# Edge tiles turned on VectorE in square blocks instead of on TensorE, with own shares' sums in PSUM and strip heads added in parts

## The chip, the core and the metric

The kernel runs on one core of a Trainium2 chip (trn2). The core's engines each have a queue of their own: TensorE (PE for its matmuls, PEld for its weight loads), VectorE (DVE), ScalarE (ACT), GpSimd (POOL) and SyncE (SP). ACT and SP also issue plain DMAs; POOL issues the indirect ones, which gather rows by an index. The metric is the device time of one execution in microseconds (us). A single execution was also recorded by the profiler; all stages and rows below are from that one.

## The reference

A graph layer over N = 50,000 nodes and 1,650,000 edges (800,000 random edges, both ways, and one loop edge for each node), sorted by destination. A node has D = 160 numbers: 64 scalars and 32 vectors of three. An edge has four numbers `sh`.

```python
s, v = x[:, :64], x[:, 64:].reshape(n, 32, 3)
ss, vv = s[src], v[src]
e0, e1 = sh[:, 0:1], sh[:, 1:4]
out0 = C0 * (ss * e0 @ W1 + einsum('eui,ei->eu', vv, e1) * INV3 @ W2)
out1 = C1 * (p3(ss, e1, W3) + p4(vv * e0, W4) + p5(cross(vv, e1), W5))
m_agg = segment_sum(concatenate([out0, out1]), dst, n)
h = concatenate([m_agg[:, :64] @ Ws, m_agg[:, 64:] by Wv])
x = layernorm(x + (x + relu(h)))
```

All of this is linear in x[src] times one of the four numbers of `sh`. So the kernel sums, for each destination and each k of 0 to 3, sh_k * x[src], and multiplies the sums by four prepared 160x160 matrices (BWk) once for each node.

## The kernel before, in words

**Groups, pairs, chunks.** Edges are cut into groups of G = 6 x 128 edges in the order of their destinations. A group touches at most W = 32 neighbouring nodes. Two groups are a pair (PG = 2, twelve blocks of 128 edges). SG = 20 groups are a chunk of ten pairs. There are 105 chunks and 1,044 pairs.

**A pair.** `gather` (L351) issues on POOL one indirect DMA for each block of 128 edges: 128 rows of x into `xg`, by the indices `si`. `spread` makes on DVE a one-hot matrix of the 32 nodes (`hot`, L360) and its product with the four numbers (`ha`, L363). `group_sums` (L388) multiplies on PE: the 128 columns of `ha` (4 numbers x 32 nodes) by the gathered rows, summed in PSUM over the six blocks of a group. `turn_sums` turns these sums on DVE in square blocks of 32x32 (L400) and adds them into a strip of nodes, `ring` (L407). `xg` has four buffers of twelve blocks, so POOL can be up to 48 gathers ahead of PE.

**A chunk.** While the ten pairs of a chunk run, the next chunk's edges are brought in. `load` (L259) issues on ACT's queue one DMA that puts the chunk's 120 blocks of 128 edges into SBUF, a block on each partition, six numbers for each edge: source, destination, four of `sh`. (For the first five chunks three DMAs from the inputs, L265 to L267; their integers are turned into floats by ACT, L274.) `place` is a generator that is taken forward in steps between the pairs' instructions, from the fifth pair on. Its steps:

- DVE picks the destination of each group's first edge (`first`, L320), PE spreads it over the partitions by a matmul with ones (L322) into PSUM (`bank`), and DVE takes it from there (`baseB`, L324); `aim` (L286 to L297) makes from it where in the strip each group's sums go.
- PE turns the sources (L328) and the destinations (L329) into `bank`, and each of the four numbers (L333) into `pk`, by matmuls with the identity.
- DVE makes the gathers' indices `si` (L336) and the place of each edge's node in its group, `rel` (L339), from `bank`, and two checks (L343, L344).

So `place` goes from DVE to PE, to DVE, to PE, and back to DVE. Each engine works through its queue in order: an instruction that waits holds all behind it.

**Strips.** A strip (`ring`, 98 of them) has ND = 5 parts of TW = 768 node columns; each starts 512 nodes after the last. When a group is the first of a new strip, what lies past column 512 of the old strip is added to the head of the new one: one DVE addition over 5 x 256 columns, L404. Before a strip is used, `set_own` writes the loop edges' shares into it: it multiplies (L691) and sums (L693) each node's shares `sa` to one number `sr`, multiplies the node's row by it (L694, 1280 columns), and turns the product into the strip (L698).

**Nodes.** When all groups of a block of 128 nodes are done, `block` multiplies the strip by BWk on PE (`phb`, L707, five matmuls), and DVE and ACT add x, relu and normalise (L183 to L197, with ACT's root at L192).

**Packing.** The destinations' loop edges are taken out of the edge list by VectorE: sixteen packs of 128 rows of 790 edges (L476 to L620). Each is read by ACT's queue, shifted together on DVE, and stored by SP's queue row by row at computed addresses in `edges` and `selves`, which later chunks read. ACT copies (L484 to L486, L504) and DVE's L505 begin each pack.

**What orders the work.** The order within PE, DVE, ACT and SP is the program's own, written by hand in the loop over pairs: matmuls of a pair, and after each one a share of the queued tasks (`after_pair`, `work`) and of the pack's steps. DMAs of ACT and SP go over eight completion counters in turn, both queues in one count: each DMA waits for the DMA that had its counter before.

The quoted functions follow as the program stands, with the profile's line numbers.

Of the kernel before, what the change touches and what calls it, by code (L numbers as in the profile page):

```python
# [39 lines left out]
F32 = mybir.dt.float32  # L40
# [10 lines left out]
P = 128  # L51
# [52 lines left out]
def tile_gnn_resnorm(ctx: ExitStack, tc: tile.TileContext, x, src, dst, attr, W1, W2, W3, W4, W5, Ws, Wv, out, n_edges):  # L104
# [123 lines left out]
    with tc.tile_pool(name="once", bufs=1) as once, tc.tile_pool(name="raw", bufs=2) as rawp, \  # L228
# [17 lines left out]
        nc.vector.tensor_copy(slotsP, slots)  # L246

        dq, loads = nc.sync, nc.scalar
        begun = []

        def load(s):

            q = loads if s else dq
            g0 = s * SG
            n = (min(NG, g0 + SG) - g0) * G
            if g0 >= NH:
                p0 = g0 * G * P - EH
                r6 = rawp.tile([P, P, 2 + NK], F32, name="r6")
                q.dma_start(r6[:n].rearrange("u p c -> u (p c)"),  # L259
                             edges[0, p0 * (2 + NK):(p0 + n * P) * (2 + NK)].rearrange("(u q) -> u q", u=n))  # L260
                return s, n, None, r6[:n, :, 0], r6[:n, :, 1], r6[:n, :, 2:]
            e = slice(g0 * G * P, (g0 * G + n) * P)
            ri = rawp.tile([P, 2, P], I32, name="ri")
            ra = rawp.tile([P, P, NK], F32, name="ra")
            q.dma_start(ri[:n, 0, :], src1[e].rearrange("(u p) o -> u (p o)", p=P))  # L265
            q.dma_start(ri[:n, 1, :], dst1[e].rearrange("(u p) o -> u (p o)", p=P))
            q.dma_start(ra[:n].rearrange("u p k -> u (p k)"), attr[e].rearrange("(u p) k -> u (p k)", p=P))  # L267
            return s, n, ri, None, None, ra[:n]

        def cast(loaded):  # L270
            s, n, ri, sf, df, af = loaded
            if ri is not None:
                rf = rawp.tile([P, 2, P], F32, name="rf")
                begun.append(nc.scalar.copy(rf[:n], ri[:n]))  # L274
                sf, df = rf[:n, 0, :], rf[:n, 1, :]
            return s, n, sf, df, af
# [37 lines left out]
        def place(cast_):  # L314

            s, n, sf, df, af = cast_
            ng = n // G

            first = idxp.tile([P, SG], F32, name="first")
            nc.vector.tensor_scalar(first[:n], starts[:n], df[:, 0:1], None, op0=ALU.mult)  # L320
            yield 1
            nc.tensor.matmul(bank[:, 3, :ng], ones[:n], first[:n, :ng], start=True, stop=True)  # L322
            baseB = idxp.tile([P, SG], F32, name="baseB")
            nc.vector.tensor_scalar(baseB[:, :ng], bank[:, 3, :ng], float(N - 1), None, op0=ALU.min)  # L324
            aim(s, ng, baseB)
            yield 1
            pi = bank[:, 1:3, :]
            nc.tensor.transpose(pi[:, 0, :n], sf, ident[:n, :n])  # L328
            nc.tensor.transpose(pi[:, 1, :n], df, ident[:n, :n])  # L329
            yield 1.5  # L330
            pk = psK.tile([P, NK, P], F32, name="pk")
            for k in range(NK):
                begun.append(nc.tensor.transpose(pk[:, k, :n], af[:, :, k], ident[:n, :n]))  # L333
                yield 0.75
            si = idxp.tile([P, P], I32, name="si")
            nc.vector.tensor_scalar(si[:, :n], pi[:, 0, :n], 0.0, float(N - 1), op0=ALU.max, op1=ALU.min)  # L336
            rel = idxp.tile([P, P], F32, name="rel")

            nc.vector.scalar_tensor_tensor(  # L339
                rel[:, :n].rearrange("p (g j) -> p g j", j=G), pi[:, 1, :n].rearrange("p (g j) -> p g j", j=G),  # L340
                float(N - 1), baseB[:, :ng].unsqueeze(2).to_broadcast([P, ng, G]),
                op0=ALU.min, op1=ALU.subtract)
            nc.vector.tensor_reduce(extremes[:, 0, s:s + 1], rel[:, :n], axis=AX.X, op=ALU.min)  # L343
            begun.append(nc.vector.tensor_reduce(extremes[:, 1, s:s + 1], rel[:, :n], axis=AX.X, op=ALU.max))  # L344
            placed[s] = si, rel, pk
# [50 lines left out]
        def turn_sums(p, ps):  # L396
# [4 lines left out]
            for i in range(ng):  # L401
                k = seg_of[g + i]
                if k and g + i == first_of[k]:
                    nc.vector.tensor_tensor(ring[k][:, :, :TW - S], ring[k][:, :, :TW - S], ring[k - 1][:, :, S:],  # L404
                                            op=ALU.add)
# [282 lines left out]
        def set_own(k, bs, got):  # L688

            xr, sa, nq = got  # L690
            nc.vector.tensor_tensor(sa[:, :nq], sa[:, :nq], quarter.unsqueeze(1).to_broadcast([P, nq, NK]), op=ALU.mult)  # L691
            sr = ownp.tile([P, BP * P // W], F32, name="sr")
            nc.vector.tensor_reduce(sr[:, :nq], sa[:, :nq], axis=AX.X, op=ALU.add)  # L693
            nc.vector.tensor_tensor(xr[:, :nq], xr[:, :nq], sr[:, :nq].unsqueeze(2).to_broadcast([P, nq, D]), op=ALU.mult)  # L694
# [23 lines left out]
        starts = once.tile([P, SG], F32, name="starts")  # L718
        nc.gpsimd.iota(starts, pattern=[[G, SG]], base=0, channel_multiplier=-1, allow_small_or_imprecise_dtypes=True)
        nc.vector.tensor_scalar(starts, starts, 0.0, None, op0=ALU.is_equal)  # L720
# [14 lines left out]
        nc.vector.scalar_tensor_tensor(quarter, quarter, float(W), of_k, op0=ALU.is_lt, op1=ALU.mult)  # L735
# [333 lines left out]
```

## Time and profile before

| what | value |
|---|---|
| time, median of 9 runs | 18,972.84 us (18,937.79 to 18,985.79) |
| profiled execution, its own time | 18,977.5 us |
| its span, first to last instruction | 18,975.8 us, so 1.7 us lie around it |
| mean granted TensorE clock in it | 0.611 |
| DVE busy | 7,102.3 us, 11,647 instructions |
| ACT busy | 224.4 us, 479 instructions |
| DMA | 805,153 packets, 1,339.61 MB, mean 71 GB/s |
| PE busy in `place`: L322, L328, L329, L333 (100 chunks) | 59.6, 46.2, 39.6, 138.0 us |
| DVE: turning of the pair's sums, L400 | 1,043 of 320 columns, 508 ns each |
| DVE: addition into the strip, L407 | 2,087 of 160 columns, 328 ns each |
| DVE: strip's head, L404 | 97 of 1,280 columns, 1,473 ns each |

How to read it: busy times are of one engine each and lie beside each other, so they don't add up to the span. What counts is which engine's queue is never ahead of the others, and what ends its waits. In a timeline a row has its start, its length, the engine, the line, the operation, out<-in and shapes; in brackets stand the engine's idle time before the row and what released it. "issue" means that nothing in the profile explains the idle time, "remote" that the releasing event has no instruction beside it.

### The profile page before, as it was taken

The numbers are of one execution on the slowest core, as the hardware profiler recorded it, in microseconds if no ns is written. First come the engines' busy times: TensorE is split into PE (matmuls) and PEld (weight loads), VectorE is DVE, ScalarE is ACT, GpSimd is POOL, SyncE is SP. The second block draws the span as 40 slices with busy tenths as digits, with TensorE's granted clock in tenths as the row PEclk, the third lists the DMA queues.
The fourth block names the chain that finished last, engine by engine and source line by source line (L and its number), as shares of the span: only waits on it lengthen the run. The fifth ranks groups of instructions, "written<-read, shape, count | busy, mean of one in ns | idle before, by whom it ended". The sixth has DMA issues, their size and how long they took to land. (4 is left out here: it accounts for less than half of the span.)

```text
span 18975.8 us, 100935 instructions
## 1 busy us (share of the span) xinstructions
PE 6943.1 (37%) x29811; PEld 5884.6 (31%) x29812; DVE 7102.3 (37%) x11647; ACT 224.4 (1%) x479; POOL 12067.8 (64%) x12536
## 2 busy tenths in 40 slices
PE   3333343333333334343433434334343333433333
PEld 3233232323323233332333323233232332323333
DVE  5342534325243343433425234252342534325223
ACT  0000000000000000000000000000000000000000
POOL 6566565665656566565665656666566665666666
PEclk6666666666566665666666666566565666656666
DMA  2222222222222222222222222222222222222222
GB/s 70 66 73 75 67 71 72 70 75 67 69 69 73 71 69 72 70 74 69 70 74 71 72 68 73 69 70 72 68 74 71 71 70 69 73 69 71 70 72 65
DMA packets 805153, 1339.61 MB, mean 71 GB/s; under 512 B 255167, under 2 KB 559476, under 8 KB 800610
## 3 DMA queue, kind: packets, MB, share of 16 engines
q0 software_dynamic: 601056, 1026.60, 20.6%
q10 hardware_dynamic: 192525, 267.12, 5.3%
q1 hardware_dynamic: 11017, 39.39, 0.6%
q8 instruction: 238, 3.90, 0.1%
q14 instruction: 317, 2.60, 0.0%
HBM read 1260.80 MB, written 71.40 MB: 70 GB/s over the span
## 5 line engine op out<-in xcount | busy, mean ns | idle before, releaser
L351 POOL DMA_INDIRECT xg<-in_x,si x12522 | 12064.0, 963 | 6886.8 <-issue 3663.5
L388 PE MATMUL ps<-xg,ha 128*128 128x160 f32 x25044 | 6185.8, 375 | 8958.2 <-issue 8314.4
L388 PEld LDWEIGHTS ps<-xg,ha 128*128 128x128 f32 x25044 | 5046.2, 246 | 9816.3 <-issue 9187.5
L400 DVE STREAM_TRANSPOSE sums<-ps 128x320 f32<-128x320 f32 x1044 | 530.1, 508 | 6332.4 <-remote 3189.5
L363 DVE TENSOR_TENSOR ha<-hot,pk 128x1536 f32<-128x1536 f32 x1044 | 1830.0, 1753 | 50.7 <-DVE hot L360 9.5
L707 PE MATMUL phb<-BWk,ring 128*128 128x160 f32 (+1 forms) x3910 | 1192.8, 375 | 1179.7 <-issue 1176.0
L707 PEld LDWEIGHTS phb<-BWk,ring 128*128 128x128 f32 (+1 forms) x3910 | 881.4, 249 | 1299.2 <-issue 1297.4
L183 DVE SCALAR_TENSOR_TENSOR y<-phb,xt 128x160 f32<-128x160 f32 x391 | 124.5, 319 | 2731.1 <-remote 1363.8
L407 DVE TENSOR_TENSOR ring<-ring,sums 128x160 f32 x2087 | 684.4, 328 | 277.0 <-issue 191.7
L505 DVE TENSOR_TENSOR hit<-marks,prow 128x395 f32<-128x395 f32 (+1 forms) x32 | 27.0, 843 | 1675.3 <-ACT marks L504 1664.6
L360 DVE TENSOR_TENSOR hot<-bank,rel 128x384 f32<-128x384 f32 x1044 | 564.7, 541 | 0.0
L322 PE MATMUL bank<-first,ones 120*128 120x20 f32 (+1 forms) x210 | 60.2, 369 | 1295.5 <-DVE first L320 738.7
L698 DVE STREAM_TRANSPOSE ring<-xr 128x1280 f32<-128x1280 f32 x188 | 466.2, 2480 | 6.4
L322 PEld LDWEIGHTS bank<-first,ones 120*128 120x128 f32 (+1 forms) x210 | 48.4, 287 | 1341.8 <-DVE first L320 765.9
L568 DVE COPY_PREDICATED prow<-marks,prow 128x2370 f32<-128x2370 int32 (+8 forms) x160 | 444.6, 2779 | 1.1
L192 ACT ACTIVATE rstd<-mv,eps_t 128x1 f32<-128x1 f32 x391 | 115.1, 294 | 16990.9 <-DVE mv L187 7468.3
L568 DVE COPY_PREDICATED pra<-marks,pra 128x1580 f32<-128x1580 int32 (+8 forms) x160 | 305.3, 1908 | 0.0
L694 DVE TENSOR_TENSOR xr<-xr,sr 128x1280 f32<-128x1280 f32 x188 | 280.0, 1489 | 6.9 <-issue 0.4
L328 PE MATMUL bank<-ident,r 120*128 120x120 f32 x100 | 46.5, 465 | 548.6 <-issue 272.7
L328 PEld LDWEIGHTS bank<-ident,r 120*128 120x128 f32 x100 | 21.1, 211 | 574.2 <-issue 284.1
L197 DVE TENSOR_SCALAR o<-y,mv,rstd 128x160 f32<-128x160 f32 x391 | 146.0, 373 | 17.7 <-DVE rstd L196 1.5
L404 DVE TENSOR_TENSOR ring<-ring 128x1280 f32<-128x1280 f32 x97 | 142.9, 1473 | 1.8
(354 smaller groups left out, 2337.9 us busy)
## 6 DMA issues: line engine op xcount, KB each, us to landing
xg<-in_x,si POOLq DMA_INDIRECT x12522
xr<-in_x ACTq DMA_DIRECT2D x748, 160.0 KB
edges<-prow SPq DMA_DIRECT2D x1994, 18.5 KB
r<-edges ACTq DMA_DIRECT2D x99, 360.0 KB
selves<-mine SPq DMA_DIRECT2D x1992, 0.5 KB
xt<-in_x ACTq DMA_DIRECT2D x195, 160.0 KB
out<-o ACTq DMA_DIRECT2D x195, 160.0 KB
pra<-in_attr ACTq DMA_DIRECT2D x15, 1580.0 KB
```

The source lines that it names most:

```text
L197: nc.vector.tensor_scalar(o[:n], y[:n], mv[:n, 0:1], rstd[:n], op0=ALU.subtract, op1=ALU.mult)
L351: nc.gpsimd.indirect_dma_start(out=xg[:, j, :], out_offset=None, in_=x, in_offset=bass.IndirectOffsetOnAxis(ap=placed[0][:, u + j:u + j + ...
L360: nc.vector.tensor_tensor(hot[:, :n], slotsP[:, 0:W].unsqueeze(1).to_broadcast([P, n, W]), rel[:, u:u + n].unsqueeze(2).to_broadcast([P, n ...
L363: nc.vector.tensor_tensor(ha[:, :n], hot[:, :n].unsqueeze(2).to_broadcast([P, n, NK, W]), pk[:, :, u:u + n].rearrange("p k u -> p u k").un ...
L388: mm = nc.tensor.matmul(ps[:, j // G, :], ha[:, j].rearrange("p k w -> p (k w)"), xr, start=j % G == 0, stop=j % G == G - 1)
L400: nc.vector.transpose(at[:, :ng], ps[:, :ng].rearrange("p g (b f) -> p g b f", f=FB))
L404: nc.vector.tensor_tensor(ring[k][:, :, :TW - S], ring[k][:, :, :TW - S], ring[k - 1][:, :, S:], op=ALU.add)
L407: nc.vector.tensor_tensor(here, here, at[:, i], op=ALU.add)
L568: nc.vector.copy_predicated(what[:n, a:e], mi[:, r].unsqueeze(2).to_broadcast([n, e - a, what.shape[2]]), what[:n, a + d:e + d])
L694: nc.vector.tensor_tensor(xr[:, :nq], xr[:, :nq], sr[:, :nq].unsqueeze(2).to_broadcast([P, nq, D]), op=ALU.mult)
L698: nc.vector.transpose(ring[k][:, :, c0:c0 + nq * W].rearrange("p b (w q) -> p q b w", q=nq), xr[:, :nq].rearrange("p q (b f) -> p q b f", ...
L707: wrote("misc", nc.tensor.matmul(ph[:nb], ring[k][:, i, c0:c0 + nb], BWk[:, i, :], start=i == 0, stop=i == ND - 1))
```

## The change

- `load` brings each chunk into SBUF in another form. The chunk's rows are cut into 30 partitions of four blocks, and each block into four quarters of 32 edges; quarter i lies on the partitions from 32 i on, by a DMA of its own. A fifth to eighth DMA bring the destination of each group's first edge (20 numbers of four bytes each, on the partitions from 32 i on). So a chunk takes eight DMAs on ACT's queue where it took one (sixteen where it took three, for the first five chunks). The tiles are made once, two of each, and cleared at the start (ten memsets on DVE) instead of coming from a pool.
- `place` uses DVE alone: three square-block transposes (32 columns for the first edges into `baseB`, 256 columns for sources and destinations into `bank`, 512 for the four numbers into `pk`) take the place of the multiplication L320, the matmul L322 and the six PE transposes of L328, L329 and L333. Its steps weigh 3 instead of 6.5 in the share of the tasks.
- `set_own`: the mask `quarter` and the sums `sr` lie in PSUM, in unused columns of `bank` (`shareP`, `sumP`).
- `turn_sums`: the strip's head is added in five additions, one for each part, and only up to the last column that the old strip's groups can have written. By the plan's bounds this is 133 to 256 columns, 215 in the mean.

```diff
         def load(s):
-            q = loads if s else dq
+            qs = [loads] * NK if s else [dq, loads] * (NK // 2)
...
+            def fetch(to, what, c):
+                rows = what.rearrange("(l b q) -> l b q", l=nl, b=nb)
+                for i, q in enumerate(qs):
+                    q.dma_start(to(slice(i * W, i * W + nl)), rows[:, :, i * W * c:(i + 1) * W * c])
+            def fetch_first(to, what, at, c):
+                firsts = what.rearrange("(g q) -> g q", g=ng)[:, at:at + 1]
+                for i, q in enumerate(qs):
+                    q.dma_start(to[i * W:i * W + ng], firsts)
...
-                q.dma_start(r6[:n].rearrange("u p c -> u (p c)"), edges[...].rearrange("(u q) -> u q", u=n))
+                fetch_first(fd, e, 1, 2 + NK)
+                fetch(lambda r: r6[r, :nb].rearrange("l b e c -> l b (e c)"), e, 2 + NK)
...
         def place(cast_):
-            nc.vector.tensor_scalar(first[:n], starts[:n], df[:, 0:1], None, op0=ALU.mult)
-            yield 1
-            nc.tensor.matmul(bank[:, 3, :ng], ones[:n], first[:n, :ng], start=True, stop=True)
-            nc.vector.tensor_scalar(baseB[:, :ng], bank[:, 3, :ng], float(N - 1), None, op0=ALU.min)
+            nc.vector.transpose(baseB, fd.to_broadcast([P, W]))
+            nc.vector.tensor_scalar(baseB[:, :ng], baseB[:, :ng], float(N - 1), None, op0=ALU.min)
             aim(s, ng, baseB)
             yield 1
-            nc.tensor.transpose(pi[:, 0, :n], sf, ident[:n, :n])
-            nc.tensor.transpose(pi[:, 1, :n], df, ident[:n, :n])
-            yield 1.5
+            nc.vector.transpose(pi[:, :, :nb * W].rearrange("p c (l b) -> p c b l", b=nb), ef)
+            yield 1
-            for k in range(NK):
-                begun.append(nc.tensor.transpose(pk[:, k, :n], af[:, :, k], ident[:n, :n]))
-                yield 0.75
+            begun.append(nc.vector.transpose(pk[:, :, :nb * W].rearrange("p k (l b) -> p k b l", b=nb),
+                                             af.rearrange("p b e k -> p k b e")))
+            yield 1
...
         def turn_sums(p, ps):
-                    nc.vector.tensor_tensor(ring[k][:, :, :TW - S], ring[k][:, :, :TW - S], ring[k - 1][:, :, S:],
-                                            op=ALU.add)
+                    past = max(high[first_of[k - 1]:first_of[k]]) + W - k * S
+                    for b in range(ND):
+                        nc.vector.tensor_tensor(ring[k][:, b, :past], ring[k][:, b, :past], ring[k - 1][:, b, S:S + past],
+                                                op=ALU.add)
...
         def set_own(k, bs, got):
-            nc.vector.tensor_tensor(sa[:, :nq], sa[:, :nq], quarter.unsqueeze(1).to_broadcast([P, nq, NK]), op=ALU.mult)
-            nc.vector.tensor_reduce(sr[:, :nq], sa[:, :nq], axis=AX.X, op=ALU.add)
-            nc.vector.tensor_tensor(xr[:, :nq], xr[:, :nq], sr[:, :nq].unsqueeze(2).to_broadcast([P, nq, D]), op=ALU.mult)
+            nc.vector.tensor_tensor(sa[:, :nq], sa[:, :nq], shareP.unsqueeze(1).to_broadcast([P, nq, NK]), op=ALU.mult)
+            nc.vector.tensor_reduce(sumP[:, :nq], sa[:, :nq], axis=AX.X, op=ALU.add)
+            nc.vector.tensor_tensor(xr[:, :nq], xr[:, :nq], sumP[:, :nq].unsqueeze(2).to_broadcast([P, nq, D]), op=ALU.mult)
```

## The prediction, on record before the changed kernel ran

> **What bounds the kernel now.** First I read the page's busy times and its costliest groups, to find the engine that never rests long.
>
> ```profile
> PE 6943.1 (37%) x29811; PEld 5884.6 (31%) x29812; DVE 7102.3 (37%) x11647; ACT 224.4 (1%) x479; POOL 12067.8 (64%) x12536
> ...
> L351 POOL DMA_INDIRECT xg<-in_x,si x12522 | 12064.0, 963 | 6886.8 <-issue 3663.5
> L388 PE MATMUL ps<-xg,ha 128*128 128x160 f32 x25044 | 6185.8, 375 | 8958.2 <-issue 8314.4
> ```
>
> POOL is the busiest, and nearly all of it is the gather. Its plain step is the median gather, 949 ns (the gather's own view), and 0.30 us of "issue" before it (the timelines below): 12,522 x 1.2535 = 15,696 us. That is 83% of the span and no part of the change touches it. The other 3,280 us are what an edit can win: gathers that last longer, and idle time above 0.3 us. The waits of POOL name what ends its idle time:
>
> ```profile
> POOL xg L351 <- issue: 3663.5, 12010, 0.7
> POOL xg L351 <- PE ps L388: 2357.4, 235, 84.8
> POOL xg L351 <- remote: 762.7, 172, 8.6
> ```
>
> The 12,010 issues are the plain step. The rest is POOL without a free `xg` buffer, waiting for PE's sums. Sorted by length, fifteen gaps are 64 to 85 us each, 1,133 us in all; they lie at the beginnings of packs, where DVE's L505 waits for ACT, and ACT's DMAs wait for SP's row-by-row stores. The change leaves that chain in place. About 380 gaps of 0.4 to 20 us hold 1,942 us above the 0.3. PE is not short of peak work in them: its largest idle time is 8,314 us of "issue", a PE that goes forward one instruction in 0.7 or 1.4 us while POOL gathers and DVE rests. It is back at pace 3 to 5 us after POOL stops, which is why a gap costs 5 us on average.
>
> **Part 1: own shares' sums in PSUM, the strip head in parts.** A timeline shows what a long DVE addition does to a gather:
>
> ```profile
> 10440.51 0.94 POOL L351 DMA_INDIRECT xg<-in_x,si  x1 [0.30 <-issue]
> ...
> 10441.61 1.49 DVE L404 TENSOR_TENSOR ring<-ring 128x1280 f32<-128x1280 f32 x1
> 10441.76 2.17 POOL L351 DMA_INDIRECT xg<-in_x,si  x1 [0.30 <-issue]
> ...
> 10444.23 0.94 POOL L351 DMA_INDIRECT xg<-in_x,si  x1 [0.30 <-issue]
> ```
>
> The gather that starts inside L404 ends 0.83 us after it and lasts 2.17 instead of 0.95 us. I sorted all gathers by the DVE row in which they start. In L404, 100 slow gathers carry 63.1 us above 0.95; in L694, 184 carry 110.9. These two have both inputs in SBUF. The others show no such rows: 179 gathers start inside the turn L698, all near 0.95, and 69 lie over L582, which has an operand in PSUM, at 0.94 to 0.95. L407, of L404's kind but 328 ns, costs about nothing.
>
> ```profile
> L698 DVE STREAM_TRANSPOSE ring<-xr 128x1280 f32<-128x1280 f32 x187 | 464.9, 2486 | 6.4
> L694 DVE TENSOR_TENSOR xr<-xr,sr 128x1280 f32<-128x1280 f32 x187 | 279.2, 1493 | 6.8 <-issue 0.4
> L404 DVE TENSOR_TENSOR ring<-ring 128x1280 f32<-128x1280 f32 x97 | 142.9, 1473 | 1.8
> ```
>
> *L694 with an operand in PSUM* becomes L582's kind (1,800 ns for 1,580 columns, so about 1,458 for 1,280: DVE's own time stays). I take all of its **-111 us**; bounds 0 (POOL makes nothing of it) and -111. *L404 in five parts*: 215 columns take 0.25 us by L404's own rate (1.15 ns a column) and 0.44 by L407's (2.05). A gather started in a part is held by at most that, and one strip head falls on about one gather, so I leave 100 x 0.2 = 20 us of 63: **-43 us**; bounds 0 and -63. DVE's five parts take 1.25 to 2.2 us for 1.47.
>
> The Trainium skill ("SBUF — State Buffer", section "Who interferes with whom") says that an operation of VectorE with two SBUF inputs contends only with a GpSimd operation that reads SBUF, and reports a probe in which tensor_tensor did not stall DMAs. By that rule both edits would be worth 0, and the sum below 18,761. The 2.17 us row above, and its hundreds of like, speak for a hold; I go by the row.
>
> **Part 2: `place` without TensorE.** Now `place` goes DVE, PE, DVE, PE, DVE. In one chunk's timeline:
>
> ```profile
> 10719.13 0.95 POOL L351 DMA_INDIRECT xg<-in_x,si  x1 [0.30 <-issue]
> 10725.96 0.33 DVE L183 SCALAR_TENSOR_TENSOR y<-phb,xt 128x160 f32<-128x160 f32 x1 [22.64 <-remote]
> ...
> 10726.78 0.20 DVE L320 TENSOR_SCALAR first<-starts,r 120x20 f32<-120x20 f32 x1
> ...
> 10727.04 0.62 PE L322 MATMUL bank<-first,ones 120*128 120x20 f32 x2 [34.14 <-DVE first L320]
> ...
> 10732.03 0.95 POOL L351 DMA_INDIRECT xg<-in_x,si  x1 [11.95 <-PE ps L388]
> ```
>
> DVE waits 22.64 us in L183 for PE's `phb`, whose end reaches it late; `first` stands behind it; PE stands 34.14 us at L322 for `first` with gathered rows lying ready; POOL runs out of buffers and stops for 11.95 us. The view of L322 says how common that is:
>
> ```profile
> its engine sat idle before it (us, times) until:
>   DVE first L320: 1504.6, 103
> ```
>
> 15 us in each chunk, of which the buffers (48 gathers ahead) cover most. What POOL loses I get by sorting its gaps by the pair of the chunk: `place` runs while PE is at the fifth to eighth pair, and POOL, up to four pairs ahead, shows it in its last pair. That pair loses 390 us in 73 gaps over all chunks; the other nine lose 172 us on average. The excess is 218 us. Counted otherwise: the gaps in which PE's next work was L322, L328, L329 or L333, or DVE's next was L336, are 44 with 290 us; all gaps with any `place` row within 25 us are 93 with 480. I take **-220 us**; bounds 0 (the same slow PE makes POOL wait a little later) and -480.
>
> *What DVE gets for it*: transposes of 32 + 256 + 512 = 800 columns a chunk, at 1.59 ns a column (L400: 508/320) to 1.94 (L698: 2,486/1,280), so 1.3 to 1.6 us, less L320's 0.2; 105 chunks make 110 to 150 us more of DVE. DVE idles 62% of the span and POOL does not wait for `si` but for buffers: **0**. Without that cover it would be +150. The matmuls that go are 283 us of PE; PE isn't late by its work, 0.
>
> **Part 3: the loads.** One DMA a chunk becomes eight, all on ACT's queue ahead of whatever ACT does next. ACT's DMA rows in the same timelines take 0.33 to 0.56 us, 7 x 0.47 = 3.3 us a chunk. Behind them on ACT stands the root L192, on which DVE's L196 waits in order, and behind L196 the turning and `hot`, `ha` for PE. L192 is issued a pair ahead of L196, 12 x 1.2535 = 15 us, so 3.3 us hide: **0**. Bounds: 0 and the price in the fourth rival. The bytes are nearly the same, in 560 pieces a chunk in place of 120: some 46,000 more beside 805,153 packets, on DMA engines that the page shows two tenths busy: 0.
>
> **Part 4: start.** Ten memsets, 3,076 columns at L655's 0.88 ns (1,125/1,280), 2.7 us before the first load, against one iota less: **+3**; bounds 0 and +10 (sixteen DMAs for the first chunk, half on SP).
>
> **Sum**: -111 - 43 - 220 + 0 + 0 + 3 = -371. From the profiled execution's 18,977.5: **18,606 us**. That execution lies 4.7 us above the median of nine, which is nothing beside the bounds.
>
> **Rivals.**
>
> 1. *All the gaps near `place` go, and the hold wholly*: -480 - 111 - 63 + 3 = -651, 18,327. For it: once PE stays ahead, POOL's buffers start each pack fuller. Against it: other pairs lose 172 us each without `place`, so some of the 93 gaps are the ordinary kind. 0.07.
> 2. *Only the holds go.* PE still creeps while POOL gathers and DVE rests; the 34 us that it stood at L322 are then spent creeping, and POOL stops in the next pair. -111 - 43 + 3 = -151, 18,827. For it: DVE's L183 waits 22 us for `phb` in both kernels, and PE goes no faster for having no L322. Against it: the last pair's excess over the other nine. 0.24.
> 3. *The change does not do what it says* for time: the holds come from something that goes with L694 and L404, and the gaps come back: 18,940 to 19,015 (0.2%, 38 us, is about what a measurement of this kernel can tell from no change). 0.07.
> 4. *Slower: ACT is held by its own loads.* ACT's and SP's DMAs take eight counters in turn, and each waits for the one that had its counter before; in the program 313 of 872 load DMAs follow one of SP's, where it was 34 of 100. SP issues its stores every 0.7 to 2.1 us while POOL gathers. A load of eight then holds ACT 3.3 + 3 x 2.1 = 9.6 us. If L192 stands behind it and less than a pair of slack is left, DVE stops at L196, PE creeps on, and POOL stops; at half of 9.6 for each of 105 chunks that is +504, and it decides from the point where ACT's hold passes the 15 us between L192 and L196. Where it decides, the gains of part 2 are given back too: +504 - 151 = +353, 19,330; with part 2 kept, +133, 19,110. For it: L196 has waited 66.7 us for ACT once already. Against it: ACT is busy 1%, and its DMA waits are shorter than a pair nearly everywhere. 0.18.
>
> **How the numbers follow.** The forecast, 18,480 to 18,720 around 18,606, has 0.44, with rival 1 0.07, rival 2 0.24: faster 0.75. Within 0.2%: 0.07. Slower: 0.18. For 8 in 10 I leave out most of rival 1 below 18,390 and the dearer part of rival 4 above 19,060. The one-sign part (faster) reaches from 18,327 to 18,935.
>
> **What would show it.** Gathers over 0.98 us that start inside the own shares' product: 184 before, a few after; at strip heads about 100 with 0.2 us in place of 0.63. POOL's last pair of a chunk should lose about 172 us like the others, and no idle of PE should be put down to `place`. DVE should be 110 to 150 us busier, its first wait in `place` one for a DMA. I am wrong if POOL's waits for PE's sums keep their 2,357 us (rival 2), if DVE's L196 waits for ACT in many chunks or the transposes wait for their loads (rival 4), or if a gather's median moves from 0.949 or its issue from 0.30: a hundredth of a microsecond there is 125 us.

## The result, and the profile after

The changed kernel took 19,072.38 us (median of 10 runs, 19,038.28 to 19,111.52), the kernel before beside it 18,983.8 us (31 runs). The ratio is 1.0051, 95% interval 1.0043 to 1.0059: **0.5% slower** (89 us), where 2% faster was forecast. The profiled execution has a span of 19,087.7 us, 111.9 more than before; it lies 17 us above its median.

The page's busy times and costliest groups, as shown of before:

```profile
PE 6958.6 (36%) x28971; PEld 5891.2 (31%) x28972; DVE 7262.7 (38%) x12254; ACT 224.7 (1%) x484; POOL 11911.4 (62%) x12535
...
L376 POOL DMA_INDIRECT xg<-in_x,si x12522 | 11907.7, 951 | 7133.7 <-issue 3664.7
L413 PE MATMUL ps<-xg,ha 128*128 128x160 f32 x25044 | 6305.7, 379 | 10823.4 <-issue 10012.0
```

POOL is busy 156 us less (the holds, gathers that last longer beside a VectorE operation, are gone), and idles 247 us more. PE's idle time of "issue", most of it in slow stretches in which PE goes forward one instruction in 0.7 or 1.4 us, grew by 1,698 us. The waits of POOL:

```profile
POOL xg L376 <- issue: 3664.7, 12005, 1.8
POOL xg L376 <- PE ps L413: 2603.7, 270, 87.1
POOL xg L376 <- remote: 736.6, 169, 7.1
```

The wait for PE's sums, which was to shrink by some 220 us, grew by 246.

Every gather's length and the idle time before it can be sorted into classes that add up to the span: 12,522 plain steps (up to 0.949 us and 0.305 before it, some 15,679 us in both), what gathers last beyond that (holds), gaps of 0.4 to 20 us, the fifteen long gaps at the beginnings of packs, and the two ends.

| us | before | after | difference |
|---|---|---|---|
| holds | 201.0 | 43.8 | -157.2 |
| gaps of 0.4 to 20 us | 1,937.5 (380) | 2,115.4 (417) | +177.9 |
| holds and those gaps together | 2,138.5 | 2,159.2 | +20.7 |
| fifteen gaps at pack beginnings | 1,128.2 | 1,206.9 | +78.7 |
| ahead of the first gather | 8.4 | 12.5 | +4.1 |
| behind the last gather | 20.6 | 28.0 | +7.4 |
| plain steps and rest | 15,680.1 | 15,681.1 | +1.0 |

The holds went as forecast (154 us), and came back as gaps. What stays is the pack beginnings and the ends.

An own shares' product of the kernel after, in its timeline, beside two gathers:

```profile
3108.89 1.49 DVE L720 TENSOR_TENSOR xr<-xr,bank 128x1280 f32<-128x1280 f32 x1
...
3109.08 0.94 POOL L376 DMA_INDIRECT xg<-in_x,si  x1 [0.30 <-issue]
...
3110.33 0.95 POOL L376 DMA_INDIRECT xg<-in_x,si  x1 [0.30 <-issue]
```

With one operand in PSUM the same 1.49 us hold neither gather, and none of the 351 gathers that lie over such a product. So why did POOL not gain? A slow stretch of the kernel after shows it:

```profile
4847.20 0.38 PE L733 MATMUL phb<-BWk,ring 128*128 128x160 f32 x1 [0.45 <-issue]
...
4857.78 0.52 DVE L425 STREAM_TRANSPOSE sums<-ps 128x320 f32<-128x320 f32 x1 [9.36 <-PE ps L413]
...
4889.35 0.33 DVE L183 SCALAR_TENSOR_TENSOR y<-phb,xt 128x160 f32<-128x160 f32 x1 [30.33 <-PE ps L413]
...
4889.88 0.94 POOL L376 DMA_INDIRECT xg<-in_x,si  x1 [6.58 <-PE ps L413]
```

PE's last `phb` matmul begins at 4,847.20. DVE, which waits for it in L183, goes on at 4,889.35, 42 us later, and within a microsecond of that POOL is let go, after 6.58 us of rest. **PE's ends reach the other engines late, and they arrive when POOL rests.**

The trace also records PE's signals themselves, the updates of the semaphore that its matmuls raise. In this stretch none is recorded from 4,857.76 to 4,889.33, though eight matmuls that raise it end in between; then fourteen come 0.04 us apart, while POOL rests. The whole trace of before has 272 such bursts (five or more updates, each at most 0.06 us behind the one before), and 264 of them begin inside one of POOL's rests of over 0.4 us, 5.6 us after its start at the median; in the trace of after it is 302 of 303. So the lateness lies between a matmul's end and its signal, not in PE's work.

One can measure it for every pair whose turning DVE had to wait for: from the end of the pair's last matmul row to the start of the turning. The median is 24.5 us in the profile of before and 26.4 us in that of after. The prediction saw "whose end reaches it late" in one row and priced PE's slow pace instead.

### The profile page after: what moved, and what is told of

It reads as the page before. It is cut to its first block, busy times and chain, and to the rows that moved or that the text cites. A ratio compares the mean times of both kernels' runs of the same rounds, so it can differ in the third digit from the quotient of the medians.

```text
span 19087.7 us, 100631 instructions
## 1 busy us (share of the span) xinstructions
PE 6958.6 (36%) x28971; PEld 5891.2 (31%) x28972; DVE 7262.7 (38%) x12254; ACT 224.7 (1%) x484; POOL 11911.4 (62%) x12535
## 3 DMA queue, kind: packets, MB, share of 16 engines
q0 software_dynamic: 601056, 1026.60, 20.3%
## 4 chain that ended last, share of the span: by engine, by line
issue 45%; POOL 31%; PE 15%; another core or an unknown queue 5%; DMA 3%; DVE 1%; DVEq 0%; ACTq 0%; POOLq 0%; ACT 0%
POOL xg L376 31%; PE ps L413 13%; DMA xg<-in_x,si 3%; PE phb L733 2%; DVE prow L595 0%; DVE ha L388 0%; DVE mine L612 0%; DVE ring L434 0%; DVE pri L592 0%; DVE hot L385 0%; DVE sums L425 0%; DVE pri L590 0%; DVE marks L588 0%; DVE ring L724 0%
## 5 line engine op out<-in xcount | busy, mean ns | idle before, releaser
L376 POOL DMA_INDIRECT xg<-in_x,si x12522 | 11907.7, 951 | 7133.7 <-issue 3664.7
L413 PE MATMUL ps<-xg,ha 128*128 128x160 f32 x25044 | 6305.7, 379 | 10823.4 <-issue 10012.0
L413 PEld LDWEIGHTS ps<-xg,ha 128*128 128x128 f32 x25044 | 5181.6, 251 | 11764.4 <-issue 10977.8
L183 DVE SCALAR_TENSOR_TENSOR y<-phb,xt 128x160 f32<-128x160 f32 x391 | 124.7, 319 | 3593.5 <-PE ps L413 2430.9
L720 DVE TENSOR_TENSOR xr<-xr,bank 128x1280 f32<-128x1280 f32 x188 | 278.8, 1483 | 7.3 <-DVE bank L719 0.7
L431 DVE TENSOR_TENSOR ring<-ring 128x196 f32<-128x196 f32 (+20 forms) x485 | 149.1, 372 | 1.8
L185 DVE BATCH_NORM_STATS2 st<-y 128x6 f32<-128x160 f32 x391 | 128.0, 327 | 13.7 <-DVE y L183 0.4
L682 DVE MEMSET ring<- 128x1280 f32 (+1 forms) x98 | 119.3, 1218 | 23.5 <-issue 21.0
L592 DVE COPY_PREDICATED_SCALAR hit<-marks,none 128x395 int32 (+8 forms) x160 | 105.0, 656 | 10.6 <-DVE pri L590 4.7
L357 DVE STREAM_TRANSPOSE pk<-r 128x512 f32<-128x512 f32 x100 | 104.5, 1045 | 0.0
```

What stands on the lines that cost most here:

```text
L376: nc.gpsimd.indirect_dma_start(out=xg[:, j, :], out_offset=None, in_=x, in_offset=bass.IndirectOffsetOnAxis(ap=placed[0][:, u + j:u + j + ...
L413: mm = nc.tensor.matmul(ps[:, j // G, :], ha[:, j].rearrange("p k w -> p (k w)"), xr, start=j % G == 0, stop=j % G == G - 1)
L431: nc.vector.tensor_tensor(ring[k][:, b, :past], ring[k][:, b, :past], ring[k - 1][:, b, S:S + past], op=ALU.add)
L720: nc.vector.tensor_tensor(xr[:, :nq], xr[:, :nq], sumP[:, :nq].unsqueeze(2).to_broadcast([P, nq, D]), op=ALU.mult)
```

## Experiments

Theory A: POOL does not set the pace; what it wins it gives back in a wait. Theory B, the prediction's: POOL sets it, and holds are on the path. Theory C: the loads of eight DMAs cost time at the pack beginnings. Each group of runs was on one chip with its own runs of the kernel before, and differences are against those. In the third group the kernel before took 15,982 us in place of some 19,000, with the same program; that difference is a finding, told below. Of the kernel before there are two traces in all, the first one and r1, so the traces of the other groups are compared with a kernel before of another group.

| run | time, before beside it | ratio, 95% interval | holds | gaps of 0.4 to 20 | pack gaps | turning behind the last matmul, median |
|---|---|---|---|---|---|---|
| e1 | 19,067.2, 19,087.4 | 0.9990 (0.9979 to 1.0001) | 97 | 2,138 | 1,144 | 22.3 |
| e2 | 19,101.6, 19,087.4 | 1.0011 (1.0000 to 1.0021) | 151 | 2,088 | 1,130 | 23.6 |
| e3 | 19,186.1, 19,087.4 | 1.0052 (1.0038 to 1.0065) | 192 | 2,028 | 1,259 | 27.2 |
| e4 | 19,150.7, 19,087.4 | 1.0035 (1.0023 to 1.0048) | 198 | 2,056 | 1,182 | 23.9 |
| r1 | 19,013.4, 19,054.7 | one run | 207 | 1,990 | 1,128 | 23.6 |
| r2 | 19,122.9, 19,054.7 | 1.0039 (1.0025 to 1.0053) | 43 | 2,170 | 1,217 | 25.8 |
| e5 | 19,087.7, 19,054.7 | 1.0022 (1.0012 to 1.0031) | 39 | 2,199 | 1,169 | 26.4 |
| e6 | 19,316.9, 19,054.7 | 1.0145 (1.0127 to 1.0163) | 201 | 2,194 | 1,167 | 26.5 |
| e7 | 16,446.9, 15,982.0 | 1.0291 (1.0274 to 1.0309) | 699 | 50 | 0 | 0.04 |
| e8 | 15,954.1, 15,982.0 | 0.9983 (0.9973 to 0.9992) | 194 | 64 | 0 | 0.04 |
| e9 | 15,834.9, 15,982.0 | 0.9907 (0.9891 to 0.9924) | 39 | 90 | 0 | 0.04 |
| r3 | 19,162.9, 19,067.8 | 1.0048 (1.0034 to 1.0063) | 41 | 2,222 | 1,252 | 25.5 |
| e10 | 19,059.8, 19,067.8 | 0.9992 (0.9982 to 1.0001) | 602 | 1,631 | 1,139 | 26.5 |
| e11 | 19,041.9, 19,067.8 | 0.9989 (0.9977 to 1.0000) | 209 | 1,815 | 1,258 | 30.8 |
| e12 | 19,100.2, 19,067.8 | 1.0016 (1.0003 to 1.0028) | 47 | 1,992 | 1,306 | 35.7 |
| e13 | 18,995.0, 18,982.4 | 1.0007 (0.9997 to 1.0016) | 39 | 2,129 | 1,160 | 20.3 |
| e14 | 18,981.5, 18,982.4 | 0.9995 (0.9985 to 1.0004) | 199 | 1,950 | 1,115 | 24.7 |
| r4 | 19,080.1, 18,982.4 | 1.0046 (1.0032 to 1.0060) | 41 | 2,108 | 1,189 | 26.6 |

(us. Pack gaps: all gaps of 20 us and more; e3, r2, r3, e11 and e12 have a sixteenth, of 20 to 35 us, and e6 has 32.)

### The parts alone

**e1**, the kernel before with the own shares' sums (and their mask) in PSUM:

```diff
-            sr = ownp.tile([P, BP * P // W], F32, name="sr")
-            nc.vector.tensor_reduce(sr[:, :nq], sa[:, :nq], axis=AX.X, op=ALU.add)
+            nc.vector.tensor_reduce(sumP[:, :nq], sa[:, :nq], axis=AX.X, op=ALU.add)
```

> The kernel before with one edit: mask and sums of the own shares in PSUM. Both theories expect the own shares' product to hold no gather (111 us of excess in 184 gathers before, about 0 here). Theory A, given back: POOL is always let go by PE, so time that POOL wins at a hold is idle time at the next empty buffer; the gaps of 0.4 to 20 us grow from 1,942 by some 80 to 130 us and the time stays within 30 us of before. Theory B, the holds are on the path: the gaps stay within 40 us of 1,942 and the time falls by 90 to 120 us.

Measured: holds 97 us, 20 us faster, with 0 just inside the interval. A is closer; B's 90 to 120 us are out.

**e2**, the kernel before with strip heads in five additions:

```diff
-                    nc.vector.tensor_tensor(ring[k][:, :, :TW - S], ...
+                    for b in range(ND):
+                        nc.vector.tensor_tensor(ring[k][:, b, :past], ...
```

> The kernel before with one edit: strip heads added in five parts, up to the last column written. Both theories expect the excess of gathers at strip heads to fall from 63 to some 40 us. Theory A (given back): time within 25 us of before. Theory B (on the path): 15 to 45 us faster.

Measured: holds 50 us less than before's 201; the time 14 us longer, not shorter. B is out here too.

**e3**, the changed kernel with those two parts taken back (the diffs above, reversed):

> The changed kernel with own shares' sums and strip heads as before, so the new loads and the placing on VectorE alone. Theory A (holds are given back): 70 to 110 us slower than before, as slow as the whole change; gaps of 0.4 to 20 us near 1,950 to 2,050, the fifteen gaps at pack beginnings some 80 us longer in all. Theory B (the holds did pay 150 us, and the placing costs what hides that): about 240 us slower than before. A third, that the placing pays its 220 us and something in the other part costs: faster than before.

Measured: 99 us slower, as the whole change. A holds, B's 240 us are out, and so is the third, that the placing pays.

**e4**, the kernel before with seven DMAs more for each load, into tiles nobody reads:

```diff
+                    for i in range(NK):
+                        q.dma_start(fx[s % 2][i * W:i * W + ng], firsts)
...
+                for i in range(1, NK):
+                    q.dma_start(rx[s % 2][i * W:i * W + nl, :nb].rearrange("l b e c -> l b (e c)"), ...)
```

> The kernel before, with seven more DMAs at each load of a chunk from the sixth on (three quarters and four columns of first edges, into a scratch tile that nothing reads). Theory C, the loads hold ACT at the beginnings of packs, where POOL already stands: the fifteen gaps there grow from 1,128 by 60 to 90 us and the time by as much, the other gaps stay within 60 us. Rival: ACT's queue is hidden there too, time within 30 us of before.

Measured: 63 us slower. The loads alone carry about two thirds of e3's cost; the rest, 35 us, is within what the two intervals leave open. The pack gaps grew by 54 us over the first profile of before, at the edge of what C asked; the gaps of 0.4 to 20 us are 118 us above that profile, where C allowed 60, but e1 and e2 of the same group, without the loads, have them as long (2,138 and 2,088).

### Where the loads cost, and whether a busy VectorE helps

**r1** is the kernel before, **r2** the changed kernel.

> The kernel before once more, for a trace from the same chip as the other runs of this group: holds of some 200 us, gaps of 0.4 to 20 us as in the three parts tried alone (2,020 to 2,140 us), fifteen gaps at pack beginnings near 1,130.

> The changed kernel once more beside it. Theory A with C: 70 to 100 us slower; against the trace of before holds 155 us less, gaps at pack beginnings 80 us more, gaps of 0.4 to 20 us up to 170 us more, of them the last pair of the chunk 150 us less and the first two pairs 200 us more: what the placing no longer costs comes back one pair later.

Measured: as expected but for the tenth pair in r2. Holds 165 less, gaps 181 more, long gaps 89 more. POOL's loss by pair of the chunk, of the first two profiles (before; after): 130, 48, 284, 230, 104, 214, 221, 157, 160, 390; and 196, 212, 270, 231, 150, 222, 207, 183, 210, 235 us. The tenth pair gave back 155 us, and the first two pairs of the next chunk, while PE, three pairs behind POOL, has just left the placing, took 230. Between r1 and r2 the first two pairs took 209 us more, but the tenth gave back only 50 where 150 were expected (306 to 256).

**e5**, the changed kernel with the loads two pairs later:

```diff
-                raws[s + 1] = load(s + 1)
-                after_pair(p + 1, do_cast, s + 1)
+                after_pair(p + 3, do_cast, s + 1)
...
+            if p % per == 2 and s + 1 < NSC:
+                raws[s + 1] = load(s + 1)
```

> The changed kernel with each chunk's loads issued at the third pair of the chunk in place of the first, so behind ACT's copies at the beginning of a pack. Theory C (the eight loads stand ahead of those copies): 50 to 85 us faster than the changed kernel, so within 40 us of before, the fifteen gaps back to 1,110 to 1,150. Rival (the loads cost something else, their packets or the counters): as slow as the changed kernel.

Measured: 35 us faster than r2, still 33 slower than before: half of what C asked, and the pack gaps stayed 41 us above r1. So the place of the loads is not all of it. In a pack's beginning of the kernel after, ACT's queue has these rows:

```profile
8953.79 1.49 ACTq L278 DMA_DIRECT2D fd<-edges  x4
8955.32 3.69 ACTq L271 DMA_DIRECT2D r<-edges  x4
8959.05 1.03 ACTq L707 DMA_DIRECT2D xr<-in_x  x2
8960.12 0.44 ACTq L819 DMA_DIRECT2D out<-o  x1
8960.66 1.58 ACT L511 CAST prow<-pri 128x790 f32<-128x790 int32 x1 [133.83 <-DMA r<-edges]
```

Of before, at the same pack:

```profile
8885.99 0.34 ACTq L259 DMA_DIRECT2D r<-edges  x1
8886.36 4.12 ACTq L680 DMA_DIRECT2D xr<-in_x  x2
```

Eight loads stand 5.2 us on ACT ahead of the copies that DVE waits for, where before had one of 0.34; but there the DMAs behind it took 4.12 us in place of 1.03. From SP's last store to ACT's first copy it is 1.65 us in the mean of the fifteen, against 1.1 before: 8 us in all. The larger part lies ahead of that: when POOL stops, SP still has 136 row stores to issue in the mean, against 127 before (131 in e4, 134 in e5, 133 in r2), at 0.44 us each. Nine more make 4 us, fifteen times some 57. Together that is 65 of the 79 us; in e4, by the same count, some 32 of 54. By the traces, 736 of SP's DMAs follow one of ACT's on their counter, where it was 606 (e4: 678, e5: 706). That SP falls behind by waiting for the loads fits most of these numbers, but no run here took that wait away alone: it is argued, not shown.

**e6**, the kernel before with ten memsets a pair on DVE:

```diff
                 if j == 1 and turning:
+                    for _ in range(10):
+                        nc.vector.memset(idle, 0.0)
                     turn_sums(*turning)
```

> The kernel before, with ten memsets of 512 columns (about 4.5 us) on VectorE ahead of each turning of a pair's sums; nothing reads them. Theory D, PE goes slowly because VectorE rests: PE's slow stretches shrink from 7.4 ms by a third or more, gaps of 0.4 to 20 us with them, and the time falls by 300 us or more. Rival, VectorE rests because PE goes slowly: the slow stretches stay at 7 ms or more and the time is equal or up to 300 us longer.

Measured: 262 us slower. PE's idle pieces of 0.15 to 3 us, which make up its slow stretches, fell from r1's 7,344 us to 5,346, by 27%; but the gaps grew, from 1,990 to 2,194 us, and the turning starts 26.5 us behind the last matmul, no earlier than before. DVE's rest is not what makes PE's ends late: theory D falls.

### Two conditions

**e7**, the kernel before with one more addition of two SBUF inputs for each pair:

```diff
                     turn_sums(*turning)
+                    nc.vector.tensor_tensor(idle, idle, idle, op=ALU.add)
```

> The kernel before, with one more VectorE addition of two SBUF inputs and 960 columns (about 1.1 us) for each pair, into a tile that nothing reads: holds of gathers are added where there were 200 us, by an estimate some 350 us more in all. Theory A (PE sets the pace, holds come out of POOL's waiting): holds and gaps of 0.4 to 20 us keep their sum within 100 us of 2,200, and the time grows by less than 130 us. Theory B (POOL sets the pace): the gaps keep their 1,990 us and the time grows by all that the holds do, 300 us or more.

**e8** and **e9**, before and after without every second matmul of the sums:

```diff
             for j, xr in enumerate(rows):
+                if j % 2:
+                    yield ps
+                    continue
```

> The kernel before without the matmuls of every second block of edges, which leaves half of the edges out of the sums. POOL's gathers, DVE's and ACT's work stay. Theory A: PE has half as many instructions to bring through a slow stretch, so the gaps of 0.4 to 20 us fall from 1,990 to under 1,200 and the time by 600 to 1,700 us. Theory B: PE's work is hidden, the time stays within 100 us of before.

> The changed kernel without the matmuls of every second block, so with half of the edges left out, too; to be compared with the run above. Theory A: with PE off the path, POOL keeps what the change gives it, so the 155 us of holds that go are won, against some 80 us at the pack beginnings: 30 to 130 us faster than the kernel before with half the matmuls, where the whole change was 70 to 90 us slower. Rival: the order stays, 60 us or more slower than that kernel.

Measured: this group met another condition. The kernel before took 15,982 us, and no trace has a slow stretch or a pack gap. Of e7, the page's rows:

```profile
L353 POOL DMA_INDIRECT xg<-in_x,si x12522 | 12541.3, 1002 | 3869.1 <-issue 3592.5
L390 PE MATMUL ps<-xg,ha 128*128 128x160 f32 x25044 | 9495.2, 499 | 5785.5 <-DMA xg<-in_x,si 4128.4
...
L402 DVE STREAM_TRANSPOSE sums<-ps 128x320 f32<-128x320 f32 x1044 | 534.5, 512 | 5350.0 <-PE ps L390 5349.6
```

PE now waits for gathered rows, not for "issue", and DVE follows the last matmul in 0.04 us. PE's signals come singly; none of the three traces has a burst. Here theory B is right: the added holds, 500 us more than e8's, cost 465, and with half the matmuls the change gains 119 us (e9 against e8; its holds are 155 less). What A foretold of e8 could not be seen, as PE was not slow.

**r3, e10, e11, e12**: the changed kernel and e7, e8, e9 once more.

> The changed kernel once more. In the last group of runs the kernel before took 15,982 us where it had taken 19,000 to 19,090, and no trace of that group has slow stretches of PE or gaps of POOL at pack beginnings. If this group is like that one, theory A now says that POOL sets the pace and the change pays: 155 us of holds less, 4 more at the start, so 80 to 160 us faster than before. If it is like the earlier ones: 70 to 100 us slower. Rival, that the change costs its 80 us wherever it runs: slower in both.

> The kernel before with the extra VectorE addition for each pair again, 500 us of holds more. Where PE has slow stretches, theory A: holds and gaps of 0.4 to 20 us together grow by less than a third of what the holds do, time by less than 200 us; theory B: by 400 us or more. Where it has none, as in the last group: some 460 us longer by both.

> The kernel before without every second matmul of the sums again, half of the edges left out. Where PE has slow stretches, theory A: 600 us or more faster than before; theory B: within 100 us. Where it has none: some 30 us faster by both, as in the last group.

> The changed kernel without every second matmul of the sums, half of the edges left out, beside the run above. Where PE has slow stretches, theory A: if half of the instructions keep PE out of POOL's way, 30 to 130 us faster than the run above; if slow stretches still end in gaps of POOL, within 60 us of it. Where it has none: 100 to 140 us faster than the run above, as in the last group.

Measured, where PE's ends come late again: the program of e7, which cost 465 us there, costs nothing here (8 us faster, interval with 0 in it). Its page:

```profile
L353 POOL DMA_INDIRECT xg<-in_x,si x12522 | 12442.7, 994 | 6589.1 <-issue 3687.3
L390 PE MATMUL ps<-xg,ha 128*128 128x160 f32 x25044 | 6478.7, 387 | 9371.6 <-issue 8302.6
...
L402 DVE STREAM_TRANSPOSE sums<-ps 128x320 f32<-128x320 f32 x1044 | 530.0, 508 | 5591.4 <-remote 3076.4
```

Holds are 602 us, some 400 more than the kernel before has in its traces, gaps 1,631: together 2,233, as without the added holds. That is A at its plainest. But A's own mechanism, PE's count of instructions, fell with e11. Half the matmuls gave 26 us where 600 were foretold:

```profile
POOL xg L351 <- PE ps L391: 1919.3, 132, 99.6
POOL xg L351 <- remote: 1187.7, 213, 12.5
```

POOL waits for PE as long as ever (3,107 us in these two rows, 3,120 in the first profile of before), though PE has half to do; its ends come 30.8 us late. And e12 is 58 us slower than e11: with PE relieved the change does not pay either. So it is the late ends, not PE's work, that set the pace.

### Would more depth ride it out, and are the two edits free?

**e13**, the kernel before with the edits of e1 and e2 together. **e14**, the kernel before with a fifth buffer:

```diff
-tc.tile_pool(name="rows", bufs=4)
+tc.tile_pool(name="rows", bufs=5)
```

(and the pools `ahead`, `outs` and `sums` one buffer shorter). **r4**, the changed kernel.

> The kernel before with both edits that take holds away, and loads and placing as before. Where PE's ends reach the others late (25 us at the median in the traces so far): holds fall by 155 us, gaps grow by about as much, the time stays within 0.2% of before, so 70 us or more ahead of the changed kernel. Where they come in time (0.04 us in the group that had the kernel before at 15,982 us): 100 to 160 us faster than before. Rival, that the holds alone cost nothing and the loads no more: as slow as the changed kernel.

> The kernel before with five buffers of gathered rows for four (three pools one buffer shorter to make room). If POOL only lacks depth to ride out the late ends (rival): its gaps of 0.4 to 20 us, one in 30 gathers, come once in 42 or more, 500 us go, the time falls by 300 us or more. Theory A, that the late ends come only when POOL rests, whatever the depth: holds and gaps keep 1,900 to 2,250 us and the time stays within 100 us.

> The changed kernel beside the two above. Where PE's ends come late: 70 to 100 us slower than before. Where they come in time: 60 to 140 us faster.

Measured: e13 0.07% over before and r4 0.46%: the two edits are free, the loads and the placing are not. In e13's waits of POOL most of the 160 us of holds have turned into waits for PE (145 us more in these two rows than in e14 below, which keeps its holds):

```profile
POOL xg L352 <- PE ps L389: 2451.8, 250, 90.3
POOL xg L352 <- remote: 801.6, 181, 8.6
```

The fifth buffer moved nothing: 1 us, with its waits as in the kernel before:

```profile
POOL xg L351 <- PE ps L388: 2374.4, 241, 88.3
POOL xg L351 <- remote: 734.3, 170, 9.6
```

Depth does not help, as A said. No complete kernel here beats the kernel before clear of its interval. e13 is level with it there, and has no holds to pay where PE's ends come in time; that it gains there is argued from e7 and e9, it was not run.

## Why the prediction was wrong

**"That is 83% of the span and no part of the change touches it. The other 3,280 us are what an edit can win."** This is the step that failed. It takes POOL's plain step for the pace and every hold and gap for a loss of its own. In the late condition holds and gaps are one sum, and what goes from one comes back in the other. By groups on one chip the sums are 2,139 and 2,159 us (before, after); 2,235, 2,239, 2,221 and 2,254 (e1 to e4, with holds from 97 to 198); 2,197, 2,213 and 2,238 (r1, r2, e5); 2,263 and 2,233 (r3, and e10 with its holds of 602); 2,168, 2,149 and 2,149 (e13, e14 with a fifth buffer, r4). Only half the matmuls (2,024 and 2,039) and ten memsets a pair (2,395) lie outside, and neither made the kernel faster by more than 26 us. What the runs show in place of that step: the pace is set by PE's late signals, which come through when POOL rests, and 400 us of added holds cost nothing (e10: 8 us faster). That a hold serves as such a rest is the reading that fits the sums; why POOL has to rest at all stays open.

**Part 1, -111 and -43.** As holds the sizes were about right: no slow gather at L720, 12 us of excess left at the strip heads where 20 were forecast, and 157 us less in all where 154 were. (The prediction counts 179 gathers that start inside L698; by the trace it is 367, four of them over 0.98 us, so the reading stands.) The Trainium skill ("SBUF — State Buffer", "Who interferes with whom") has a VectorE operation with two SBUF inputs contend with a GpSimd operation that reads SBUF. The prediction took the gather for one that doesn't, and so read no holds out of the rule; but the gather takes its indices `si` from SBUF, and by the same words holds could be expected. The runs decide it: e7 added 1,044 such additions, and its holds were 500 us above e8's. As time the -154 was 0 in the late condition (e13: +13, interval -6 to +30 us), and would have been close to right in the other (e7, e9).

**Part 2, -220.** The tenth pair did fall from 390 to 235 us, and no wait for `first` is left. But the other nine went from 1,548 to 1,881. What was read as "15 us in each chunk" was counted double: the 1,504.6 us of L322's view add the waits of the matmul and of its weight load, which are the same time.

```profile
PEld bank L322 <- DVE first L320: 765.9, 52, 49.9
PE bank L322 <- DVE first L320: 738.7, 51, 49.1
...
L322 PE MATMUL bank<-first,ones 120*128 120x20 f32 (+1 forms) x210 | 60.2, 369 | 1295.5 <-DVE first L320 738.7
```

PE stood 766 us for `first`, in half of the chunks. Whatever it waited for, it idled 1,296 us before L322 and 568 before L328. Both are gone, 1,864 us, and PE's idle time before the sums' matmuls grew by 1,865 us, from 8,958 to 10,823: not a microsecond of it was won. Rival 2 had said this: "the 34 us that it stood at L322 are then spent creeping, and POOL stops in the next pair." It erred in keeping the -154 of the holds. Rival 3 ("the gaps come back") had the end of the holds right, by luck: its reason was that something else makes them. DVE's transposes took more than forecast:

```profile
L357 DVE STREAM_TRANSPOSE pk<-r 128x512 f32<-128x512 f32 x100 | 104.5, 1045 | 0.0
...
L354 DVE STREAM_TRANSPOSE bank<-r 128x256 f32<-128x256 f32 x100 | 63.4, 634 | 0.2 <-issue 0.2
...
L349 DVE STREAM_TRANSPOSE baseB<-fd 128x32 f32<-128x32 f32 x105 | 20.9, 199 | 1.9 <-ACT fd L303 1.6 <-issue 0.3
```

That is 1.88 us a chunk, 2.0 to 2.5 ns a column in place of 1.59 to 1.94 in the larger two. DVE's busy time grew by 160 us, where 110 to 150 were forecast. That it cost nothing is likely but was not shown apart from the loads (e3 less e4 is 35 us).

**Part 3, 0.** Put at nothing, and e4 measures +63 (0.23% to 0.48%). Rival 4 named the counters and the sign, but put the price at L196 in every chunk. The traces put it at the pack beginnings, which the prediction had set aside as a "chain in place": 1,128 us became 1,207. L196 waited 67.2 us for the root in all, 0.5 us more than before.

**Part 4, +3.** Measured +4.1.

**Why not seen.** The profile of before had the lateness in its rows: L183's 22.64 us of "remote", POOL's 762.7 us of "remote" and, on its page, this row of the turning:

```profile
L400 DVE STREAM_TRANSPOSE sums<-ps 128x320 f32<-128x320 f32 x1044 | 530.1, 508 | 6332.4 <-remote 3189.5
```

An idle engine with no instruction beside its release was read as a slow PE. What was not measured: the time from the end of a pair's last matmul to the start of what waits for it.

## What to carry to other kernels

Before an edit is priced at the engine that seems to set the pace, add an artificial load to that engine: where 400 us of extra holds cost nothing (e10), taking holds away won nothing either (e13). Measure the time from the last instruction of a producer to its waiting consumer; where it was tens of microseconds, signals and not work set the pace here, and neither half the matmuls nor a fifth buffer helped. Plain DMAs on the queue of an engine that is 1% busy are not free: seven more a chunk cost 63 us (e4). The likely reason is that their counters are shared with another queue's backlog, so count which DMAs come to wait across queues.

## What the runs showed that was not expected

- The same program has two conditions: 15,982 us with DVE 0.04 us behind PE's last matmul, and some 19,000 (19% longer) with 20 to 36 us. The chip of the first was also that of the last group, in which the kernel before took 18,982. What makes the ends late was not found. They arrive some microseconds into a rest of POOL (its gaps of 0.4 to 20 us last 5.1 us above the plain step in the mean).
- One rival for the cause was not tested, the recording itself. The traces of the late condition also hold fewer of the DMAs' completion signals: 40,403 updates of 18,288 DMAs in that of before, 230,958 of as many in e8's. So "remote" and "issue" can there stand for a signal that was not recorded, and no execution is on record without its span and clock, so none shows what the kernel takes when nothing is recorded.
- In the late condition SP is slow as well: 0.44 us a store in the mean while POOL rests at pack beginnings, and 1.10 us at the median while it gathers (first profile of before). In e8's trace, of the other condition, it is 0.33 us at the median while POOL gathers.
- Gathers last either 945 or 948 ns on average from execution to execution, whatever the kernel: 34 us in all, which a difference of two spans must not be read without.
